# Mixture of experts: the last 128 tokens take slots behind each expert's first 128, and three quads of experts run in two passes

## The chip, the cores and the metric

One core of a Trainium2 chip runs the whole program in one launch. The metric is device time in microseconds (us) from start to end of that launch. The names of the engines in the profile: PE is TensorE (matrix products and transposes), PEld its weight loads, DVE is VectorE, ACT is ScalarE, POOL is GpSimd, SP is SyncE (it issues most DMA transfers). Each engine executes its own queue in order; the profile leaves buffer numbers out of the names of tiles.

## The reference

Six layers on x of 16 x 64 tokens by 256 channels. Five of them are untouched by this change. The last one is a mixture of experts, computed densely in the reference:

```python
def _gate(x, gate_w, gate_bias):          # 64 experts in 8 groups, 8 experts per token
    scores = jax.nn.sigmoid(x @ gate_w.T)
    sc = scores + gate_bias[None, :]
    # the 4 best groups by the sum of their two best scores; then the top 8 experts of these
    tw = jnp.take_along_axis(scores, tidx, axis=1)
    tw = tw / (tw.sum(-1, keepdims=True) + 1e-20)
    return (tidx, tw * 2.5)
def body(acc, ws):                        # once per expert
    wg, wu, wdn, cw = ws
    hmid = jax.nn.silu(x @ wg) * (x @ wu)
    return (acc + cw[:, None] * (hmid @ wdn), None)
y, _ = jax.lax.scan(body, jnp.zeros_like(x), (We_gate, We_up, We_down, w_dense.T))
shared = jax.nn.silu(hidden_states @ Ws_gate) * (hidden_states @ Ws_up) @ Ws_down
return y + shared                         # 1024 tokens, 256 channels, 128 hidden units per expert
```

## The kernel before

The kernel doesn't compute the 64 experts on all tokens. It sorts token rows by expert through two buffers in DRAM, `xbuf` and `ybuf`. The work of the last layer in order:

**Routing.** The 1024 tokens are eight groups of 128 (`NG` = 8, `P` = 128). `route(g)` normalises a group, computes scores, selects eight experts per token (`sel`, a 0/1 matrix of 128 tokens by 64 experts) and numbers the tokens of each expert. The number of a token within its expert is a sum: `before` (a triangular matrix of ones) times `sel` counts the tokens ahead of it in its own group, and `ones` times `seen` counts the tokens of all earlier groups, both accumulated in `ps_pos` (L1243 to L1246). `seen` is the running sum of `sel`. From this number comes the address of a row in `xbuf`, `idx` (L1255). `most` (L1261) is the largest count of any expert: if it were above `CAP` = 192, a dense fallback behind the loop would run. With these inputs it is not above that, before or after the change. `post` (L1160) issues GpSimd's indirect DMAs that scatter the token rows, one DMA per group and choice, 64 in all, with the list `scatters`.

**Slots.** Each expert has 192 slots. Four experts make a quad (16 quads); a quad has `NBLK` = 6 blocks of 128 rows: blocks 0 to 3 hold the first 128 slots of its four experts, block 4 the other 64 slots of its first two experts, block 5 those of the last two. Any group's tokens can land in any block.

**Experts.** `load_quad(q)` loads the weights of a quad (1.5 MB, `wq`, 5 buffers). `fetch(q)` (L1505) reads the quad's six blocks from `xbuf` into `xg` (3 buffers) in one DMA and is ordered behind all 64 scatters; it then computes on VectorE where each result row goes in `ybuf` (`mine`, `left`, `goal`). `turn(q, part)` (L1520) transposes two blocks on TensorE (four transposes) and copies them to `xT` (2 buffers): parts 0 and 1 by VectorE, part 2, the remainders, by ScalarE. `up(e)` (L1533) multiplies the gate and up weights of an expert with its 192 columns (`ps_ee`), applies Silu on ScalarE (`hg`) and multiplies on VectorE (`hT`). `down(e)` multiplies `hT` with the down weights: `ps_ey` for the first 128 slots of an expert, and for every second expert `ps_er` for the remainders of a pair, each half taking 64 partitions; results are copied to `yo` (4 buffers) and scattered to `ybuf` by GpSimd (`send`, L1547).

The loop at L1599 runs over the experts: at the start of a quad it fetches the quad after the next, in each of the next three iterations it does one part of the next quad's `turn`, then `up(e)` and `down(e - 3)`. Five quads of weights are loaded and two quads fetched ahead of it. `weights(g)` (L1581) computes the eight combine weights of a group's tokens on VectorE, four operations on 128 x 512 elements (L1584 eq, L1585 eq, L1587 w8, L1590 dgl); it is called from the same loop, every seventh expert:

```python
        if e % 7 == 3 and len(w8s) < NG:
            weights(len(w8s))
```

The order of each engine's queue is not the order of this text: a scheduler that works from dependencies and priorities places the instructions of all engines, and tile buffers add waits for the reader of an earlier tile. Behind the loop, `collect` and the code after it gather the eight result rows of each token from `ybuf` and sum them.

Of the kernel before, what the change touches and what calls it, by code (L numbers as in the profile page):

```python
# [34 lines left out]
CAP = 192  # L35
NBLK = 6
# [3 lines left out]
NOSLOT = 1 << 14  # L40

DX = D + 2 * TOPK

NAHEAD, NPE = 5, 4
BIG = 3.0e38
# [105 lines left out]
def perceiver_kernel(ctx: ExitStack, tc: tile.TileContext, a: dict, consts: bass.AP, out: bass.AP):  # L151
# [75 lines left out]
    def psb(shape, name):  # L227
        return ps_b.tile(shape, F32, tag="b", name=name)
# [3 lines left out]
    def after(i, others):  # L232
        for o in others:
            tc.add_manual_dep(i.ins, o.ins.name, mybir.DependencyInfo(mybir.DependencyClass.Sync, mybir.DependencyReason.DATA), reason="order")

# [941 lines left out]
    def route(g):  # L1177
# [23 lines left out]
        sc = tmp([P, E], "sc")  # L1201
        V.tensor_tensor(sc, sig, gb, ALU.add)


        scg = sc.rearrange("p (g k) -> p g k", k=8)
        hi, lo, n = scg, None, 4
# [33 lines left out]


        pp = psm([P, E], f"ps_pos_{g}")
        T.matmul(pp, lhsT=const2("before"), rhs=sel, start=True, stop=g == 0)  # L1243
        if g:
            T.matmul(pp, lhsT=const2("ones"), rhs=seen, start=False, stop=True)
        fit = tmp([P, E], "fit")  # L1246
        V.scalar_tensor_tensor(fit, pp, CAP - 0.5, sel, ALU.is_lt, ALU.mult)
# [8 lines left out]
        if g == NG - 1:  # L1256

            pn = psm([P, E], "ps_most")
            T.matmul(pn, lhsT=const2("ones"), rhs=seen, start=True, stop=False)
            T.matmul(pn, lhsT=const2("ones"), rhs=sel, start=False, stop=True)  # L1260
            V.reduce_max(most, pn, AX.X)  # L1261
        elif g == 0:
            V.tensor_copy(seen, sel)
        else:
            V.tensor_tensor(seen, seen, sel, ALU.add)
# [17 lines left out]
    with p2:  # L1283
# [168 lines left out]
        def shared():  # L1452
            w = loaded[0]
            wg, wu = (w[:, i * D : (i + 1) * D].rearrange("p (c f) -> p c f", c=2) for i in range(2))
            wd = w[:, 2 * D : 3 * D]
            for q in range(4):
                yield from until(lambda: sw["routed"] >= 2 * q + 2)
                tk = slice(q * 256, (q + 1) * 256)
                pe = psb([P, 2, 256], f"ps_se_{q}")
                for i, w in enumerate((wg, wu)):  # L1460
                    for c in range(2):
                        T.matmul(pe[:, i, :], lhsT=w[:, c, :], rhs=xnTm[:, c, tk], start=c == 0, stop=c == 1)
                th = wide("xth")([P, 256], f"th_s{q}")
                A.activation(th, pe[:, 0, :], AF.Tanh, scale=0.5)
# [23 lines left out]

    hid = ctx.enter_context(tc.tile_pool(name="hid", bufs=3, reuse_waits="tile"))

    wqs, xgs, goals, xTs, hTs, yos, pys = [], [], [], [], {}, {}, {}

    def wide_slot(name):
        return hid.tile([P, 4, 3 * D], F32, tag="wq", bufs=NAHEAD, name=name)
# [1 line left out]
    def load_quad(q):  # L1496

        w = wide_slot(f"wq_{q}")
        for i, n in enumerate(("gate", "up", "down")):
            v = a[f"L1_ffn_We_{n}"][4 * q : 4 * q + 4]  # L1500
            v = v.rearrange("e p d -> p e d") if i == 2 else v.rearrange("e (p c) f -> p e (c f)", c=2)
            nc.sync.dma_start(out=w[:, :, i * D : (i + 1) * D], in_=v)
        wqs.append(w)

    def fetch(q):  # L1505

        xg = hid.tile([P, NBLK, DX], F32, tag="xg", bufs=3, name=f"xg_{q}")
        after(nc.sync.dma_start(out=xg, in_=xbuf[q * QROWS : (q + 1) * QROWS, :].rearrange("(p s) d -> p s d", p=P)), scatters)
        mine = hid.tile([P, NBLK, TOPK], F32, tag="mine", bufs=2, name=f"mine_{q}")
        V.scalar_tensor_tensor(mine, xg[:, :, D : D + TOPK], float(q * QROWS), _bc(const2("own"), 2, TOPK), ALU.add, ALU.is_equal)  # L1510
        V.tensor_tensor(mine, mine, xg[:, :, D + TOPK : DX], ALU.mult)
        left = hid.tile([P, NBLK], F32, tag="left", bufs=2, name=f"left_{q}")
        V.reduce_sum(left, mine, AX.X)
        goal = hid.tile([P, NBLK], I32, tag="goal", bufs=4, name=f"goal_{q}")
        V.tensor_scalar(goal, left, -1.0, float(NOSLOT), ALU.mult, ALU.add)
        xgs.append(xg)
        goals.append(goal)
        xTs.append(hid.tile([P, 4, 2, CAP], F32, tag="xT", bufs=2, name=f"xT_{q}"))

    def turn(q, part):  # L1520

        pt = psb([P, 2, 2, P], f"ps_xT_{q}_{part}")
        xT = xTs[q]
        for s in range(2):
            for c in range(2):
                to = pt[:, c, s, :] if part == 2 else pt[:, s, c, :]
                T.transpose(to, xgs[q][:, 2 * part + s, c * P : (c + 1) * P], ident)  # L1527
        if part == 2:
            A.copy(xT[:, :, :, P:CAP].rearrange("p i c k -> p c i k"), pt.rearrange("p c s (u k) -> p c (s u) k", u=2))
        else:  # L1530
            V.tensor_copy(xT[:, 2 * part : 2 * part + 2, :, 0:P], pt)

    def up(e):  # L1533
        q, i = divmod(e, 4)
        pe = psb([P, 2, CAP], f"ps_ee_{e}")
        for j in range(2):
            for c in range(2):
                w = wqs[q][:, i, j * D + c * F : j * D + (c + 1) * F]
                T.matmul(pe[:, j, :], lhsT=w, rhs=xTs[q][:, i, c, :], start=c == 0, stop=c == 1)  # L1539
        hg = hid.tile([P, CAP], F32, tag="hg", name=f"hg_{e}")  # L1540
        A.activation(hg, pe[:, 0, :], AF.Silu)  # L1541
        hT = hid.tile([P, CAP], F32, tag="hT", bufs=5, name=f"hT_{e}")
        V.tensor_tensor(hT, hg, pe[:, 1, :], ALU.mult)
        hTs[e] = hT

    def send(y, goal):
        arr = G.indirect_dma_start(  # L1547
            out=ybuf,
            out_offset=bass.IndirectOffsetOnAxis(ap=goal, axis=0),
            in_=y,  # L1550
            in_offset=None,
            bounds_check=NTOK * TOPK - 1,
            oob_is_err=False,
        )

        if arrivals:
            tc.declare_no_dep(arr.ins, group="arrivals", reason="goals differ")
        tc.add_to_no_dep_group("arrivals", arr.ins)
        arrivals.append(arr)

    def down(e):
        q, i = divmod(e, 4)
        if i % 2 == 0:
            pys[e // 2] = psb([P, 2, D], f"ps_ey_{e}")
            yos[e // 2] = hid.tile([P, 3, D], F32, tag="yo", bufs=4, name=f"yo_{e}")
        py, yo = pys[e // 2], yos[e // 2]
        T.matmul(py[:, i % 2, :], lhsT=hTs[e][:, 0:P], rhs=wqs[q][:, i, 2 * D : 3 * D], start=True, stop=True)  # L1567
        if i % 2 == 0:
            return
        pr = psb([P, D], f"ps_er_{e}")  # L1570
        for u in range(2):
            T.matmul(pr[u * 64 : (u + 1) * 64, :], lhsT=hTs[e - 1 + u][:, P:CAP], rhs=wqs[q][:, i - 1 + u, 2 * D : 3 * D], start=True, stop=True)  # L1572
        A.copy(yo[:, 0:2, :], py)  # L1573
        V.tensor_copy(yo[:, 2, :], pr)
        for s in range(3):
            blk = i - 1 + s if s < 2 else 4 + i // 2
            send(yo[:, s, :], goals[q][:, blk : blk + 1])

# [13 lines left out]

    for q in range(NAHEAD):
        load_quad(q)
    fetch(0)
    fetch(1)
    for part in range(3):
        turn(0, part)
    for e in range(E + 3):  # L1599
        q, i = divmod(e, 4)  # L1600
        if i == 0 and q + 2 < NQUAD:
            fetch(q + 2)
        if i == 3 and q and q - 1 + NAHEAD < NQUAD:
            load_quad(q - 1 + NAHEAD)
        if e < E:
            if i < 3 and q + 1 < NQUAD:
                turn(q + 1, i)
            up(e)
        if e > 2:
            down(e - 3)  # L1610
        if e % 7 == 3 and len(w8s) < NG:
            weights(len(w8s))


# [87 lines left out]
```

## Time and profile before

| | before |
|---|---|
| median of 6 runs, us | 1088.95 (1084.83 to 1090.86) |
| profiled execution, us | 1087.79 |
| its span, first to last instruction, us | 1085.9 |
| mean granted TensorE clock | 0.915 |
| busy: PE / PEld / DVE | 858.5 (79%) / 648.6 (60%) / 632.7 (58%) |
| busy: ACT / POOL | 292.0 (27%) / 273.5 (25%) |
| `ps_ee` matmuls (L1539) | 512, 95.4 us busy |
| scatters to `xbuf` (L1163) / to `ybuf` (L1547) | 64, 69.5 us busy / 96, 93.7 us busy |
| first `ps_ee` | at 881.18 us |

Times in a timeline are microseconds from the start of the span. A row "busy, mean ns | idle before <-releaser" tells how long a group of instructions ran, and how long its engine had been idle just before them and what ended that. The experts lie from 881 to about 1043 us; the gather and the sum take the rest.

### The profile page before, as it was taken

Reading aid. Unit: us, or ns where it says so; the run is one execution under the profiler, and the core shown is the slowest. Engines: PE = TensorE matmul, PEld = TensorE weight load, DVE = VectorE, ACT = ScalarE, POOL = GpSimd, SP = SyncE. Lnnn points to the kernel's source line nnn. Section 1 sums busy time; section 2 is a strip of 40 time slices with the busy share of each in tenths; the row PEclk is TensorE's granted clock in tenths of the full one; section 3 lists DMA queues with packets and bytes.
Section 4 is the critical chain, followed back from the end, with each engine's and each line's share of the span. In section 5 each row is a group of like instructions: output and inputs, shape, how many; then the busy total and the mean of one; then the engine's idle time right before and its main releaser. Section 6 shows DMA issues by size and latency. Waiting matters only on the chain. (4 is left out here: it accounts for less than half of the span.)

```text
span 1085.9 us, 15921 instructions
## 1 busy us (share of the span) xinstructions
PE 858.5 (79%) x5858; PEld 648.6 (60%) x5858; DVE 632.7 (58%) x1863; ACT 292.0 (27%) x672; POOL 273.5 (25%) x302
## 2 busy tenths in 40 slices
PE   4878888978899788987786768877867369999945
PEld 3655565646656555655554556766766268777824
DVE  1446564565546564456556695979896853333316
ACT  0314032322233132231233454432311022232210
POOL 0000100001000101001011131575655516556540
PEclk8889999999999999999888788999998579999978
DMA  7411141310502131101501453343403859888236
GB/s 239 174 40 62 62 152 32 123 62 2 183 7 116 62 127 58 61 1 63 157 1 35 107 121 73 84 130 78 146 16 106 319 192 298 281 287 287 74 120 271
DMA packets 70725, 130.56 MB, mean 120 GB/s; under 512 B 10099, under 2 KB 56623, under 8 KB 67574
## 3 DMA queue, kind: packets, MB, share of 16 engines
q1 hardware_dynamic: 56016, 107.97, 30.6%
q0 software_dynamic: 7680, 17.33, 4.6%
q10 hardware_dynamic: 6950, 4.23, 1.4%
q8 instruction: 47, 0.77, 0.3%
q14 instruction: 32, 0.26, 0.1%
HBM read 97.54 MB, written 36.14 MB: 123 GB/s over the span
## 5 line engine op out<-in xcount | busy, mean ns | idle before, releaser
L1547 POOL DMA_INDIRECT ybuf<-yo,goal x96 | 93.7, 976 | 85.8 <-ACT yo L1573 31.1
L1539 PE MATMUL ps_ee<-xT,wq 128*128 128x192 f32 x512 | 95.4, 330 | 0.0
L1539 PEld LDWEIGHTS ps_ee<-xT,wq 128*128 128x128 f32 x512 | 81.8, 190 | 6.5 <-issue 3.5
L1163 POOL DMA_INDIRECT xbuf<-xtok,idx x64 | 69.5, 1086 | 47.9 <-issue 16.8
L994 PE MATMUL fpy<-fw,fxm 128*128 128x256 f32 x256 | 60.6, 397 | 13.3 <-DVE fxm L991 6.8
L630 PE MATMUL po_a<-cn,paT_a 128*64 128x256 f32 (+1 forms) x416 | 57.0, 410 | 15.7 <-ACT paT_a L624 7.7
L994 PEld LDWEIGHTS fpy<-fw,fxm 128*128 128x128 f32 x256 | 50.4, 199 | 24.3 <-issue 16.0
L1400 PE MATMUL ps_g<-pc,pb 128*128 128x128 f32 x384 | 55.1, 306 | 9.7 <-DVE pb L1367 6.7
L1400 PEld LDWEIGHTS ps_g<-pc,pb 128*128 128x128 f32 x384 | 53.2, 220 | 12.8 <-POOL pc L1369 10.7
L630 PE MATMUL po_b<-cn,paT_b 128*64 128x256 f32 (+1 forms) x416 | 50.2, 385 | 9.2 <-DVE paT_b L624 8.3
L208 POOL TENSOR_TENSOR rs_ff<-ve_ff,neghalf 128x1 f32<-128x1 f32 x8 | 4.4, 550 | 209.4 <-DVE ve_ff L206 197.9
L404 PE MATMUL psc<-ct,cn 128*128 128x128 f32 x384 | 49.8, 280 | 3.6 <-DVE cc_a L570 2.2
L1541 ACT ACTIVATE hg<-ps_ee 128x192 f32<-128x192 f32 x64 | 21.3, 333 | 109.0 <-PE ps_ee L1539 40.6
L592 PE MATMUL sc_b<-cT,qT_b 128*64 128x512 f32 (+1 forms) x256 | 47.3, 524 | 2.1 <-DVE qT_b L564 1.6
L630 PEld LDWEIGHTS po_a<-cn,paT_a 128*64 128x64 f32 (+1 forms) x416 | 28.5, 145 | 33.5 <-ACT paT_a L624 8.7
L404 PEld LDWEIGHTS psc<-ct,cn 128*128 128x128 f32 x384 | 44.7, 145 | 6.4 <-issue 3.2
L197 ACT COPY cT<-psc 128x512 f32<-128x512 f32 x51 | 29.8, 589 | 63.9 <-PE psc L404 63.3
L1527 PE MATMUL ps_xT<-ct,xg 128*128 128x128 f32 x192 | 30.7, 288 | 20.2 <-DMA xg<-xbuf 20.2
L592 PE MATMUL sc_a<-cT,qT_a 128*64 128x512 f32 (+1 forms) x256 | 46.4, 505 | 0.0
L630 PEld LDWEIGHTS po_b<-cn,paT_b 128*64 128x64 f32 (+1 forms) x416 | 27.7, 136 | 25.4 <-DVE paT_b L624 10.1
L208 POOL TENSOR_TENSOR rs_ml<-ve_ml,neghalf 128x1 f32<-128x1 f32 x8 | 5.6, 705 | 141.8 <-DVE ve_ml L206 141.8
L1527 PEld LDWEIGHTS ps_xT<-ct,xg 128*128 128x128 f32 x192 | 24.1, 148 | 28.7 <-DMA xg<-xbuf 20.4
(443 smaller groups left out, 1888.2 us busy)
## 6 DMA issues: line engine op xcount, KB each, us to landing
cn<-in_ctx_dram SPq DMA_DIRECT2D x16, 1536.0 KB
e<-segd SPq DMA_DIRECT2D x16, 896.0 KB
xbuf<-zero SPq DMA_DIRECT2D x8, 1632.0 KB
xg<-xbuf SPq DMA_DIRECT2D x16, 816.0 KB
wq<-in_L_ffn_We_gate_dram SPq DMA_DIRECT2D x16, 512.0 KB
wq<-in_L_ffn_We_up_dram SPq DMA_DIRECT2D x16, 512.0 KB
wq<-in_L_ffn_We_down_dram SPq DMA_DIRECT2D x16, 512.0 KB
yg<-ybuf SPq DMA_DIRECT2D x8, 1024.0 KB
```

The source lines that it names most:

```text
L197: A.copy(dst, src)
L208: root = G.tensor_tensor(rs, ve, neghalf[:, 0:1], ALU.pow)
L404: T.transpose(ps[:, j, :], cn[:, 4 * q + j, c * P : (c + 1) * P], ident)
L592: T.matmul(sc[b * 64 : (b + 1) * 64, :], lhsT=qT[:, c, b * 64 : (b + 1) * 64], rhs=cTs[2 * g + b][:, c, 512 * j : 512 * j + n], start=c == ...
L630: T.matmul(pos[j > 0][b * 64 : (b + 1) * 64, :], lhsT=paTs[j][:, i, b * 64 : (b + 1) * 64], rhs=cns[2 * g + b][0:r, k, :], start=k in (0, ...
L994: T.matmul(py, lhsT=xm[:, t, c, :], rhs=fw[:, 2 * h + t, c, :], start=h + t + c == 0, stop=h == 3 and t == 1 and c == 1,)
L1163: sct = G.indirect_dma_start(out=xbuf, out_offset=bass.IndirectOffsetOnAxis(ap=idx[:, g, k : k + 1], axis=0), in_=xtok[:, g, 0:DX], in_off ...
L1400: T.matmul(pg[:, 2 * j : 2 * j + 2, :].rearrange("p q t -> p (q t)"), lhsT=pb[:, l + i, j, :], rhs=pcs[l + i][:, j, :, :].rearrange("p q t ...
L1527: T.transpose(to, xgs[q][:, 2 * part + s, c * P : (c + 1) * P], ident)
L1539: T.matmul(pe[:, j, :], lhsT=w, rhs=xTs[q][:, i, c, :], start=c == 0, stop=c == 1)
L1541: A.activation(hg, pe[:, 0, :], AF.Silu)
L1547: arr = G.indirect_dma_start(out=ybuf, out_offset=bass.IndirectOffsetOnAxis(ap=goal, axis=0), in_=y, in_offset=None, bounds_check=NTOK * T ...
```

## The change

Three things. First, the last group's tokens are numbered from `full` = max(128, tokens of earlier groups), so that they take slots behind each expert's first 128, that is only in blocks 4 and 5. Second, the first three quads (`NSPLIT` = 3, twelve experts) are done in two passes: blocks 0 to 3, whose fetch is ordered behind the first 56 scatters only, with `up` on columns 0 to 128 and the `ps_ey` products; then blocks 4 and 5, fetched behind all scatters, into a tile of their own, with `up` on columns 128 to 192 and the `ps_er` products. The main loop starts at expert 12. Third, the first Silu is ordered behind the shared expert's last Tanh, the first send behind the last scatter in GpSimd's queue, and `weights` is called every sixth expert. The declaration with "rows" says that a first-pass fetch reads other blocks than the last group's scatters write.

```diff
+NSPLIT = 3
...
+        if g == NG - 1:                                # in route(g)
+            pn = psm([P, E], "ps_full")
+            T.matmul(pn, lhsT=const2("ones"), rhs=seen, start=True, stop=True)
+            full = tmp([P, E], "full")
+            V.tensor_scalar(full, pn, float(P), None, ALU.max)
...
-        T.matmul(pp, lhsT=const2("before"), rhs=sel, start=True, stop=g == 0)
-        if g:
+        last = g == NG - 1
+        T.matmul(pp, lhsT=const2("before"), rhs=sel, start=True, stop=last or g == 0)
+        if last:
+            pos = tmp([P, E], "pos")
+            V.tensor_tensor(pos, pp, full, ALU.add)
+            pp = pos
+        elif g:
             T.matmul(pp, lhsT=const2("ones"), rhs=seen, start=False, stop=True)
...
-            T.matmul(pn, lhsT=const2("ones"), rhs=seen, start=True, stop=False)
-            T.matmul(pn, lhsT=const2("ones"), rhs=sel, start=False, stop=True)
-            V.reduce_max(most, pn, AX.X)
+            T.matmul(pn, lhsT=const2("ones"), rhs=sel, start=True, stop=True)
+            V.tensor_tensor(full, full, pn, ALU.add)
+            V.reduce_max(most, full, AX.X)
...
-    def fetch(q):
-        xg = hid.tile([P, NBLK, DX], F32, tag="xg", bufs=3, name=f"xg_{q}")
-        after(nc.sync.dma_start(out=xg, in_=xbuf[...]), scatters)
+    def fetch(q, lo=0, hi=NBLK):                       # xg, goal: only blocks lo to hi
+        ld = nc.sync.dma_start(out=xg, in_=rows)
+        if hi == 4:
+            after(ld, scatters[:-TOPK])
+            tc.declare_no_dep(ld.ins, group="rows", keep=[o.ins for o in scatters[:-TOPK]], reason="blocks differ")
+        else:
+            after(ld, scatters)
...
+        if part == 2 and q < NSPLIT:                   # in turn(q, part)
+            xT = xTs[q] = hid.tile([P, 4, 2, CAP], F32, tag="xT", bufs=2, name=f"xTr_{q}")
...
-    def up(e):
+    def up(e, lo=0, hi=CAP):                           # only columns lo to hi
...
+        if e == 0 and lo == 0:
+            after(silu, [sw["tanh"]])
...
+        if not arrivals:                               # in send
+            behind(arr, scatters[-1])
...
-    def down(e):
+    def down(e, first=True, rest=True):                # first: ps_ey; rest: ps_er
...
-    fetch(0)
-    fetch(1)
-    for part in range(3):
-        turn(0, part)
-    for e in range(E + 3):
+    for q in range(NSPLIT):
+        fetch(q, 0, 4)
+    n = 4 * NSPLIT
+    for e in range(n + 2):
+        if e < n:
+            if e % 4 == 0:
+                turn(e // 4, 0)
+                turn(e // 4, 1)
+            up(e, 0, P)
+        if e > 1:
+            down(e - 2, rest=False)
+    for q in range(NSPLIT):
+        fetch(q, 4, NBLK)
+    for e in range(n + 2):
+        if e < n:
+            if e % 4 == 0:
+                turn(e // 4, 2)
+                if e:
+                    load_quad(e // 4 - 1 + NAHEAD)
+            up(e, P, CAP)
+        if e > 1:
+            down(e - 2, first=False)
+    load_quad(NSPLIT - 1 + NAHEAD)
+    fetch(NSPLIT)
+    fetch(NSPLIT + 1)
+    for part in range(3):
+        turn(NSPLIT, part)
+    for e in range(n, E + 3):
...
-        if i == 3 and q and q - 1 + NAHEAD < NQUAD:
+        if i == 3 and q > NSPLIT and q - 1 + NAHEAD < NQUAD:
...
-        if e > 2:
+        if e > n + 2:
             down(e - 3)
-        if e % 7 == 3 and len(w8s) < NG:
+        if e % 6 == 3 and len(w8s) < NG:
```

In a second pass `ps_er` of a pair is made in two separate iterations, one half each, where before both halves stood next to each other.

More of the change, by code (lines that the diff above doesn't have):

```diff
@@ L234, in after, with behind @@
             tc.add_manual_dep(i.ins, o.ins.name, mybir.DependencyInfo(mybir.DependencyClass.Sync, mybir.DependencyReason.DATA), reason="order")
+    def behind(i, o):
+        tc.add_manual_dep(i.ins, o.ins.name, mybir.DependencyInfo(mybir.DependencyClass.NoSync, mybir.DependencyReason.DATA), reason="order")
     def drive(*kinds):
@@ L1463, in shared @@
                 th = wide("xth")([P, 256], f"th_s{q}")
-                A.activation(th, pe[:, 0, :], AF.Tanh, scale=0.5)
+                sw["tanh"] = A.activation(th, pe[:, 0, :], AF.Tanh, scale=0.5)
                 hT = wide("xc")([P, 256], f"hT_s{q}")
@@ L1489, in perceiver_kernel @@
     hid = ctx.enter_context(tc.tile_pool(name="hid", bufs=3, reuse_waits="tile"))
-    wqs, xgs, goals, xTs, hTs, yos, pys = [], [], [], [], {}, {}, {}
+    wqs, xgs, goals, xTs, hTs, yos, pys, prs = [], [], [], [], {}, {}, {}, {}
     def wide_slot(name):
@@ L1503, in load_quad @@
         wqs.append(w)
-    def fetch(q):
-        xg = hid.tile([P, NBLK, DX], F32, tag="xg", bufs=3, name=f"xg_{q}")
-        after(nc.sync.dma_start(out=xg, in_=xbuf[q * QROWS : (q + 1) * QROWS, :].rearrange("(p s) d -> p s d", p=P)), scatters)
-        mine = hid.tile([P, NBLK, TOPK], F32, tag="mine", bufs=2, name=f"mine_{q}")
-        V.scalar_tensor_tensor(mine, xg[:, :, D : D + TOPK], float(q * QROWS), _bc(const2("own"), 2, TOPK), ALU.add, ALU.is_equal)
+    def fetch(q, lo=0, hi=NBLK):
+        if lo == 0:
+            xgs.append(hid.tile([P, NBLK, DX], F32, tag="xg", bufs=3, name=f"xg_{q}"))
+            goals.append(hid.tile([P, NBLK], I32, tag="goal", bufs=4, name=f"goal_{q}"))
+            xTs.append(hid.tile([P, 4, 2, CAP], F32, tag="xT", bufs=2, name=f"xT_{q}"))
+        xg, goal = xgs[q][:, lo:hi, :], goals[q][:, lo:hi]
+        rows = xbuf[q * QROWS : (q + 1) * QROWS, :].rearrange("(p s) d -> p s d", p=P)[:, lo:hi, :]
+        ld = nc.sync.dma_start(out=xg, in_=rows)
[4 more added lines that the diff above has]
+            after(ld, scatters)
+        mine = hid.tile([P, NBLK, TOPK], F32, tag="mine", bufs=2, name=f"mine_{q}_{lo}")[:, lo:hi, :]
+        V.scalar_tensor_tensor(mine, xg[:, :, D : D + TOPK], float(q * QROWS), _bc(const2("own")[:, lo:hi], 2, TOPK), ALU.add, ALU.is_equal)
         V.tensor_tensor(mine, mine, xg[:, :, D + TOPK : DX], ALU.mult)
-        left = hid.tile([P, NBLK], F32, tag="left", bufs=2, name=f"left_{q}")
+        left = hid.tile([P, NBLK], F32, tag="left", bufs=2, name=f"left_{q}_{lo}")[:, lo:hi]
         V.reduce_sum(left, mine, AX.X)
-        goal = hid.tile([P, NBLK], I32, tag="goal", bufs=4, name=f"goal_{q}")
         V.tensor_scalar(goal, left, -1.0, float(NOSLOT), ALU.mult, ALU.add)
-        xgs.append(xg)
-        goals.append(goal)
-        xTs.append(hid.tile([P, 4, 2, CAP], F32, tag="xT", bufs=2, name=f"xT_{q}"))
     def turn(q, part):
@@ L1531, in turn @@
             V.tensor_copy(xT[:, 2 * part : 2 * part + 2, :, 0:P], pt)
-    def up(e):
+    def up(e, lo=0, hi=CAP):
         q, i = divmod(e, 4)
-        pe = psb([P, 2, CAP], f"ps_ee_{e}")
+        pe = psb([P, 2, CAP], f"ps_ee_{e}_{lo}")[:, :, lo:hi]
         for j in range(2):
@@ L1538, in up @@
                 w = wqs[q][:, i, j * D + c * F : j * D + (c + 1) * F]
[L1539 to L1543, printed above, removed]
+                T.matmul(pe[:, j, :], lhsT=w, rhs=xTs[q][:, i, c, lo:hi], start=c == 0, stop=c == 1)
+        hg = hid.tile([P, CAP], F32, tag="hg", name=f"hg_{e}_{lo}")[:, lo:hi]
+        silu = A.activation(hg, pe[:, 0, :], AF.Silu)
+        if e == 0 and lo == 0:
+            after(silu, [sw["tanh"]])
+        hT = hid.tile([P, CAP], F32, tag="hT", bufs=5, name=f"hT_{e}_{lo}")
+        V.tensor_tensor(hT[:, lo:hi], hg, pe[:, 1, :], ALU.mult)
         hTs[e] = hT
@@ L1559, in send @@
         arrivals.append(arr)
-    def down(e):
+    def down(e, first=True, rest=True):
         q, i = divmod(e, 4)
         if i % 2 == 0:
[L1564 to L1567, printed above, removed]
+            if first:
+                pys[e // 2] = psb([P, 2, D], f"ps_ey_{e}")
+            yos[e // 2] = hid.tile([P, 3, D], F32, tag="yo", bufs=4, name=f"yo_{e}_{rest}")
+        yo = yos[e // 2]
+        if first:
+            py = pys[e // 2]
+            T.matmul(py[:, i % 2, :], lhsT=hTs[e][:, 0:P], rhs=wqs[q][:, i, 2 * D : 3 * D], start=True, stop=True)
+        if not first and i % 2 == 0:
+            prs[e // 2] = psb([P, D], f"ps_er_{e}")
+        if not first:
+            u = i % 2
+            T.matmul(prs[e // 2][u * 64 : (u + 1) * 64, :], lhsT=hTs[e][:, P:CAP], rhs=wqs[q][:, i, 2 * D : 3 * D], start=True, stop=True)
         if i % 2 == 0:
             return
[L1570 to L1575, printed above, removed]
+        if first:
+            A.copy(yo[:, 0:2, :], py)
+        if rest:
+            if first:
+                pr = psb([P, D], f"ps_er_{e}")
+                for u in range(2):
+                    T.matmul(pr[u * 64 : (u + 1) * 64, :], lhsT=hTs[e - 1 + u][:, P:CAP], rhs=wqs[q][:, i - 1 + u, 2 * D : 3 * D], start=True, stop=True)
+            else:
+                pr = prs[e // 2]
+            V.tensor_copy(yo[:, 2, :], pr)
+        for s in range(0 if first else 2, 3 if rest else 2):
             blk = i - 1 + s if s < 2 else 4 + i // 2
```

## The prediction

> **What bounds the kernel now.** I read the windows (the stretch where the gap is), then the timeline there, then the groups of the VectorE queue, then the timeline of one pair of experts at full clock for prices. First the windows from 840 us; columns: stretch, length, busy us with instruction counts of PE, PEld, DVE, ACT, POOL, granted PE clock, DMA share, GB/s.
>
> ```profile
> 850.00:858.00 8.00, 1.94 (x8) 1.78 (x8) 7.63 (x28) 0.00 (x0) 3.60 (x4) 0.50 1.08 392
> 858.00:877.00 19.00, 0.00 (x0) 0.00 (x0) 15.70 (x29) 0.00 (x0) 9.40 (x8) 0.50 0.56 192
> 879.00:881.00 2.00, 2.00 (x11) 1.90 (x9) 1.73 (x6) 0.46 (x1) 0.00 (x0) 0.54 0.80 336
> 881.00:883.00 2.00, 1.96 (x14) 1.80 (x13) 1.35 (x5) 1.63 (x3) 0.00 (x0) 1.00 0.75 238
> 896.00:916.00 20.00, 20.00 (x125) 16.73 (x125) 7.30 (x25) 5.85 (x14) 11.60 (x12) 1.00 0.89 289
> ```
>
> TensorE does nothing for 19 us while GpSimd issues the last scatters; but VectorE is busy 15.70 of those 19 us. Later, in the experts, TensorE is busy 20.00 of 20 us: there the end is set by TensorE work, so TensorE time added there is added to the kernel. The timeline of the gap (start, duration, engine, line; in brackets the idle time before and its releaser):
>
> ```profile
> 859.86 1.93 POOL L1163 DMA_INDIRECT xbuf<-xtok,idx  x1 [5.34 <-DVE idx L1255]
> ...
> 870.42 0.97 POOL L1163 DMA_INDIRECT xbuf<-xtok,idx  x1 [0.30 <-issue]
> ...
> 873.05 7.75 SPq L1508 DMA_DIRECT2D xg<-xbuf  x4
> 873.52 0.69 DVE L1590 TENSOR_TENSOR dgl<-ct,w 128x512 f32<-128x512 f32 x1
> 877.61 0.21 DVE L1510 SCALAR_TENSOR_TENSOR mine<-xg,ct 128x48 f32<-128x48 f32 x1 [3.40 <-DMA xg<-xbuf]
> 877.63 3.51 PE L1527 MATMUL ps_xT<-ct,xg 128*128 128x128 f32 x16 [20.23 <-DMA xg<-xbuf]
> ```
>
> So the first expert waits for: last idx 859.42, eight scatters to 871.39, fetch 873.05, landed 877.6. The dgl row beside it is the other thing to see. It is the last of the combine weights (`weights`), which the text of the kernel puts into the expert loop, but which VectorE executes here, in one run (VectorE groups, 849.9 to 874.3; busy us, mean ns of one, then idle before):
>
> ```profile
> L1590 DVE TENSOR_TENSOR dgl<-ct,w 128x512 f32<-128x512 f32 x8 | 5.5, 689 | 0.2
> L1585 DVE TENSOR_TENSOR eq<-eq,wt 128x512 f32<-128x512 f32 x8 | 5.5, 686 | 0.2
> ```
>
> With L1584 and L1587, equally long, these are 32 rows of 0.69 us, 22 us, ending at 874.21. In before they cost nothing: the data comes at 877.6.
>
> **The start.** After the change the first fetch waits for 56 scatters only (the last of these ended at 854.52) and can land about 4.5 us after its issue, early in the gap. TensorE turns its eight blocks, but their copy into `xT` (new line 1559) is VectorE's, and in the built order of the changed kernel the VectorE queue reads: `idx` of the last group, then 26 of the 32 `weights` rows (new L1629 to L1635), and only then `mine` (L1540), `left`, `goal` and the copy. An engine's queue is executed in order, so the first expert waits for VectorE, not for data. VectorE's work to that point is the 32 rows as before plus three new 128x64 operations (pos, full twice), at 0.13 start to start (847.60 to 847.74) about 0.3: free at 874.21+0.3 = 874.5. Then 0.9 for mine/left/goal (877.61 to 878.5 in before), 0.69 for the copy, 0.1 to TensorE: first `ps_ee` at 876.2 instead of 881.18: **-5.0**. The other bound is no `weights` rows in the way: rival A.
>
> The remainder's fetch isn't late: 5 `weights` rows fewer stand ahead of the last `idx` (6, before 11), so idx comes about 3 us earlier, 856.5, and eight scatters later (11.5 us), 868, the second fetch goes out; it is needed when the first pass ends: twelve `up` of 0.94, twelve `ps_ey` of 0.5, sixteen transposes of 0.11 and 1.7 for the clock (all below) after 876.2, that is 897. The route's extra TensorE product and the three DVE rows are in those numbers; `ps_pos` and `ps_most` each have one product fewer: 0.
>
> **Transposes.** Before, sixteen transposes were done ahead of 881.18; after, eight. The other eight at 0.11 come later: **+0.9**. In before the half clock (0.50 to 879, 0.54 to 881) ended with those transposes. After the change TensorE again comes from a gap of over 10 us, so expert work runs at half clock for the 3.4 us that the transposes needed (877.63 to 881): 0 if the early transposes count, at most half of 3.4, 1.7. I take **+1.7**, the row nearest.
>
> **The split matmuls.** Twelve experts do `up` twice, 128 and 64 columns wide, instead of once with 192. Prices at full clock:
>
> ```profile
> 801.09 2.03 PE L1357 MATMUL ps_C<-xnTm,winT 128*128 128x128 f32 x16
> 802.96 1.90 PE L1433 MATMUL ps_y<-xtok,gt 128*128 128x64 f32 x16
> 804.69 1.94 PE L1382 MATMUL ps_z<-winT,xnTm 128*128 128x512 f32 x4
> ...
> 897.99 1.47 PE L1539 MATMUL ps_ee<-xT,wq 128*128 128x192 f32 x8
> 899.29 0.59 PE L1567 MATMUL ps_ey<-wq,hT 128*128 128x256 f32 x2
> 899.82 0.65 PE L1572 MATMUL ps_er<-wq,hT 128*64 128x256 f32 x4
> 900.40 0.66 PE L1527 MATMUL ps_xT<-ct,xg 128*128 128x128 f32 x4
> ```
>
> Start to start: 192 wide, 1.30 for 8 (0.163 each); 128 wide, 1.87/16 = 0.117; 64 wide, 1.73/16 = 0.108. So 64 columns cost nearly as much as 128: each has a 128x128 weight load to go with it, and below 128 columns that load is the floor. An expert: 8 x (0.113+0.108) = 1.77 against 1.30, +0.47; twelve: **+5.6**. Bounds: +0.5 if 64 columns cost half of 128 (8 x (0.113+0.057) = 1.36 each, +0.06); +7.3 with 0.117 and a little gap each (+0.61).
>
> [...]
>
> **The rest products.** `ps_er` before: the two halves of a pair go side by side in 0.58 for four instructions (899.82 to 900.40). In the second pass another `up` stands between the halves, so each runs alone, nearest row `ps_ey`, two of 256 columns in about 0.5: 1.0 for 0.58, six pairs, **+2.4** (1.7 at 0.43, 3.0 at 0.54).
>
> **Exposed copies.** Before, the transposes of quad q+1 are spread over quad q. In the split passes they stand directly ahead of their use. First pass, quads 1 and 2: VectorE copy 0.69, partly covered by the pending `down`, 0.45 each. Second pass, three turns with ScalarE copies (0.59 plus 0.3 to and from it, and behind the `yo` copy on ScalarE): about 1.05, 0.85, 0.9. **+3.7** (2 to 5.5).
>
> **Nothing for:** ACT_TABLE_LOAD (1.28 at 881.15, begun beside the first `ps_ee`): after, it waits for that matmul's end, and `down` follows two experts later, so the second expert's matmuls and transposes cover 1.3; uncovered it is +1.4. [...] The other new waits hold nobody: the first Silu waits for the shared expert's Tanh, which was done before 846.19 (VectorE reads it there), and the first send stands behind the last scatter, over by 868, while no result exists before 880. The sends stay 96, and 11.60 of 20 us busy leaves GpSimd room. Later stage: 0, bounds in the rivals.
>
> **Sum:** -5.0+0.9+1.7+5.6+2.4+3.7 = +9.3. On the profiled 1087.79 (span 1085.9 and 1.9 around it) that is 1097.1; the median of the runs, 1088.95, stands 1.2 higher. I say 1097. A measurement of this kernel can tell about 0.3%, 3.3 us, from no change.
>
> **Rivals.**
>
> A, *it starts early as the scatters allow*: the copies aren't held by `weights`. From 854.52, 1.7 to the issue (871.39 to 873.05), 4.6 to landing (873.05 to 877.61), 1.7 to the matmul as above and one row of 0.69 in between: first `ps_ee` at 863.2 or a little later, I say 863.6, 12.6 before my 876.2. 9.3-12.6 = -3.3: 1084.5, faster. For it: data and expert weights are there. Against: the built queue, and the rows of before, which run in just such an order. It decides if the new L1540 runs before the L1629 to L1635 rows. 0.06.
>
> B, *most of it given back later*: between 916 and 1036 TensorE is idle for 5.06 us (18.24 of 20 busy in 916 to 936, DMA share 0.84), because weights and blocks arrive late. With the start spread, the queued loads get further ahead, and that idle goes: 9.3-5.1 = +4.2, 1092. The low end of the split price gives the same, 9.3-5.6+0.5 = +4.2; both together, -0.9, no change. Against the first: the transfers are as many and their buffers come free later too. 0.13.
>
> C, *slower still, one queue*: SyncE's transfers are issued in order. In the built order wq_5, wq_6, wq_7 (each waiting for a quad's second pass) stand ahead of xg_5 to xg_7; before, weights and blocks alternated (wq_5 at 895.83, an xg at 903.26). wq_7 goes out when the second pass ends, about 918; three loads of 1.5 MB at 290 GB/s are 5.4 us each, so xg_5 may land around 926, when VectorE's queue reaches its `mine`, with the copies for the next quad behind that. TensorE then waits 4 to 8: 1101 to 1105. Against: in before TensorE never lost over 1.8 in 20 us to this. It decides if xg_5 lands after 926. 0.12.
>
> **How the numbers follow.** Forecast 0.69, A 0.06, B 0.13, C 0.12. The forecast's unknowns: split +0.5 to +7.3, half clock 0 to 1.7, copies 2 to 5.5, table 0 to 1.4; not all at one end, about 1091 to 1101. The range takes in B and C: 1087 to 1105; A lies outside. Faster by over 0.3% (below 1085.7): A and a sliver of B and of the forecast's low end, 0.10. Within: most of B and the low end of the forecast, 0.13. Slower (above 1092.2): 0.77.
>
> **What would show it.** In the profile after: first `ps_ee` about 876, released by DVE xT, just after a dgl row; 128x64 `ps_ee` groups at 0.108 each; GpSimd's scatters over by 868; the first expert of quad 3 at about 919 (907.75 before). Wrong if `ps_ee` starts before 870, if 64-wide rows take under 0.08, or if TensorE's idle after 916 is not near 5.

## The result and the profile after

The changed kernel takes 1100.08 us (median of 20 runs, 1093.41 to 1109.86) against 1089.93 for the kernel before (46 runs): a ratio of 1.0087, 95% interval 1.0071 to 1.0104, which is 9.5 us more. The ratio leaves out the one slow run, 1109.86 us at a mean granted clock of 0.895. The profiled execution took 1097.9 us with a span of 1095.7, 9.8 more than before.

Because the layers ahead of the change vary from one execution to the next, I read the traces from one point on: the first `more` row of the last group on VectorE (the ranking of the expert groups in `route(7)`), "the ranking" below. It comes at 847.60 before and at 849.79 after. From there to the end of the last `ps_er` it is 196.28 us before and 204.55 after: +8.3. The 2.2 ahead of the ranking and -0.7 behind the experts make up the rest of the 9.8.

First the windows of the changed kernel, columns as before:

```profile
858.00:877.00 19.00, 1.94 (x8) 1.57 (x8) 18.28 (x34) 0.00 (x0) 8.78 (x8) 0.50 0.91 339
879.00:881.00 2.00, 2.00 (x11) 2.00 (x11) 1.39 (x10) 1.08 (x1) 0.00 (x0) 0.50 0.00 0
881.00:883.00 2.00, 2.00 (x14) 1.95 (x14) 0.57 (x2) 1.03 (x4) 0.00 (x0) 0.77 0.00 0
900.00:920.00 20.00, 18.52 (x122) 13.97 (x122) 5.12 (x23) 3.61 (x14) 6.82 (x7) 1.00 0.64 200
```

In the 19 us in which TensorE did nothing it now does eight transposes, 1.94 us. VectorE is busy 18.28 of 19 us, before 15.70. The half clock lasts 2 us longer than before. In the second pass TensorE is not even busy all the time (18.52 of 20). The timeline of the start (new line numbers: L1170 scatter, L1532 fetch, L1555 and L1559 `turn`, L1567 `up`, L1635 the last row of `weights`):

```profile
861.49 13.66 SPq L1532 DMA_DIRECT2D xg<-xbuf  x6
868.28 1.19 POOL L1170 DMA_INDIRECT xbuf<-xtok,idx  x1 [0.30 <-issue]
870.00 1.94 PE L1555 MATMUL ps_xT<-ct,xg 128*128 128x128 f32 x8 [13.69 <-DMA xg<-xbuf]
875.65 0.69 DVE L1635 TENSOR_TENSOR dgl<-ct,w 128x512 f32<-128x512 f32 x1
876.26 0.18 DVE L1540 SCALAR_TENSOR_TENSOR mine<-xg,ct 128x32 f32<-128x32 f32 x1
877.00 0.69 DVE L1559 COPY xT<-ps_xT 128x512 f32<-128x512 f32 x1
877.74 4.92 PE L1567 MATMUL ps_ee<-xT,wq 128*128 128x128 f32 x24 [5.80 <-DVE xT L1559]
879.92 1.28 ACT L1569 ACT_TABLE_LOAD   x1 [30.96 <-PE ps_ee L1567]
```

The first blocks are there at 870.0, when the last scatter has only just been issued (868.28 and 1.19); the copy that the first expert needs starts at 877.00, directly behind the last dgl row and four rows of `mine`, `left` and `goal`. TensorE's bracket says the same from the other side: 5.80 us idle, ended by VectorE's xT.

The prices of the two passes, from the timeline of TensorE at full clock, first two rows of the first pass, then of the second:

```profile
882.93 1.05 PE L1567 MATMUL ps_ee<-xT,wq 128*128 128x128 f32 x8
883.83 0.60 PE L1602 MATMUL ps_ey<-wq,hT 128*128 128x256 f32 x2
...
906.48 1.10 PE L1567 MATMUL ps_ee<-xTr,wq 128*128 128x64 f32 x8 [0.68 <-ACT xTr L1557]
907.51 0.65 PE L1607 MATMUL ps_er<-wq,hT 128*64 128x256 f32 x2
908.09 1.10 PE L1567 MATMUL ps_ee<-xTr,wq 128*128 128x64 f32 x8
```

Start to start: eight 128 columns wide 0.90, eight 64 columns wide 1.03, one half of `ps_er` 0.58. An expert's `up` costs 0.89+1.03 where before it cost 1.30.

### The profile page after: what moved, and what is told of

It is laid out like the page before. It is cut to its first block, busy times and chain, and to the rows that moved or that the text cites. A ratio compares the mean times of both kernels' runs of the same rounds, so it can differ in the third digit from the quotient of the medians.

```text
span 1095.7 us, 16171 instructions
## 1 busy us (share of the span) xinstructions
PE 874.4 (80%) x5952; PEld 661.5 (60%) x5952; DVE 637.1 (58%) x1890; ACT 295.6 (27%) x684; POOL 270.8 (25%) x302
## 4 chain that ended last, share of the span: by engine, by line
PE 50%; DVE 24%; DMA 10%; issue 8%; ACT 4%; POOL 2%; ACTq 0%; POOLq 0%; SPq 0%; another core or an unknown queue 0%; DVEq 0%
PE fpy L1001 5%; PE po_b L637 4%; PE sc_b L599 4%; PE po_a L637 4%; PE sc_a L599 4%; PE ps_ee L1567 4%; PE psc L411 3%; PE ps_g L1419 2%; POOL ybuf L1577 2%; DMA ybuf<-yo_True,goal 2%; DMA xg<-xbuf 2%; DVE pc L1388 1%; DVE gs L1229 1%; DMA x<-in_x_dram 1%; DVE gt L1427 1%
## 5 line engine op out<-in xcount | busy, mean ns | idle before, releaser
L1577 POOL DMA_INDIRECT ybuf<-yo_True,goal x84 | 81.9, 976 | 75.6 <-issue 21.5
L1567 PE MATMUL ps_ee<-xT,wq 128*128 128x192 f32 (+1 forms) x512 | 92.1, 325 | 6.8 <-DVE xT L1559 6.2
L1567 PEld LDWEIGHTS ps_ee<-xT,wq 128*128 128x128 f32 x512 | 80.5, 196 | 13.3 <-DVE xT L1559 6.8
L1170 POOL DMA_INDIRECT xbuf<-xtok,idx x64 | 67.0, 1047 | 44.2 <-issue 16.8
L1569 ACT ACTIVATE hg<-ps_ee 128x192 f32<-128x192 f32 (+2 forms) x76 | 23.2, 307 | 109.8 <-PE ps_ee L1567 75.8
L1573 DVE TENSOR_TENSOR hT<-hg,ps_ee 128x192 f32<-128x192 f32 (+2 forms) x76 | 23.7, 319 | 50.0 <-ACT hg L1569 45.6
L1555 PE MATMUL ps_xT<-ct,xg 128*128 128x128 f32 x192 | 29.8, 283 | 14.8 <-DMA xg<-xbuf 14.8
```

The lines of the kernel that those rows point to most:

```text
L1170: sct = G.indirect_dma_start(out=xbuf, out_offset=bass.IndirectOffsetOnAxis(ap=idx[:, g, k : k + 1], axis=0), in_=xtok[:, g, 0:DX], in_off ...
L1567: T.matmul(pe[:, j, :], lhsT=w, rhs=xTs[q][:, i, c, lo:hi], start=c == 0, stop=c == 1)
L1569: silu = A.activation(hg, pe[:, 0, :], AF.Silu)
L1573: V.tensor_tensor(hT[:, lo:hi], hg, pe[:, 1, :], ALU.mult)
L1577: arr = G.indirect_dma_start(out=ybuf, out_offset=bass.IndirectOffsetOnAxis(ap=goal, axis=0), in_=y, in_offset=None, bounds_check=NTOK * T ...
```

## Experiments

Every ratio below is against runs of the kernel before on the same chip; the medians themselves differ between chips (before: 1077 to 1090 us), so only ratios are compared. Times in the three right columns come from one profile each, in us.

| kernel | ratio, 95% interval | ranking to first `ps_ee` | first `ps_ee` to last `ps_er` | ranking to last `ps_er` |
|---|---|---|---|---|
| before | 1 | 33.6 | 162.7 | 196.3 |
| before, second profile | - | 32.4 | 163.7 | 196.1 |
| changed | 1.0087 (1.0071 to 1.0104) | 28.0 | 176.6 | 204.6 |
| after_wait_all | 1.0091 (1.0064 to 1.0117) | 27.8 | 178.6 | 206.4 |
| after_late | 1.0072 (1.0044 to 1.0099) | 20.9 | 178.0 | 199.0 |
| before_slots | 0.9974 (0.9954 to 0.9995) | 29.4 | 162.7 | 192.0 |
| before_late | 0.9979 (0.9956 to 1.0003) | 27.0 | 160.4 | 187.4 |
| after_pairs | 1.0185 (1.0157 to 1.0213) | 27.9 | 180.8 | 208.7 |
| after_hoist | 1.0087 (1.0058 to 1.0116) | 27.8 | 171.1 | 198.9 |
| after_wide | one run | 27.9 | 175.6 | 203.5 |
| pairs_wide | one run | 27.9 | 174.8 | 202.7 |
| p1_all | 0.9969 (0.9943 to 0.9996) | 15.9 | 172.3 | 188.2 |
| p2_hoist | 0.9980 (0.9955 to 1.0005) | 14.0 | 176.3 | 190.2 |
| p3_hoist | 1.0003 (0.9975 to 1.0032) | 16.0 | 176.9 | 192.9 |

My theory going in: VectorE's queue holds the first blocks, and the passes then cost TensorE time. The rivals: data or scatters hold them; the loss is in the routing; the loss comes later, from transfers.

### Is it the early fetch, VectorE's queue or the numbering?

**after_wait_all**: the first fetches wait for all scatters.

```diff
         if hi == 4:
-            after(ld, scatters[:-TOPK])
-            tc.declare_no_dep(ld.ins, group="rows", keep=[o.ins for o in scatters[:-TOPK]], reason="blocks differ")
+            after(ld, scatters)
```

> The changed kernel, with the first fetches ordered behind all 64 scatters instead of the first 56. Theory: VectorE is held to 876.3 anyway, and the scatters end near 869, so the fetch lands by about 876: the total moves by less than 1.5 us, that is, the early fetch as such brings next to nothing in the changed kernel. Rival (the early fetch does bring the start forward): 4 us slower or more.

```profile
873.04 1.94 PE L1554 MATMUL ps_xT<-ct,xg 128*128 128x128 f32 x8 [18.51 <-DMA xg<-xbuf]
875.87 5.49 PE L1566 MATMUL ps_ee<-xT,wq 128*128 128x128 f32 x24 [0.89 <-DVE xT L1558]
```

The timeline of TensorE in this kernel: the transposes come 25.0 us after the ranking (873.04 less 848.04), 4.8 later than in the changed kernel, and yet the first `ps_ee` stands 27.8 us after the ranking as there (28.0). The idle time in the bracket has shrunk from 5.80 to 0.89: only the wait for VectorE became shorter. The ratio is the same. Fetching early brings nothing in the changed kernel.

**after_late**: the combine weights behind the experts that they are written beside.

```diff
-        V.tensor_tensor(hT[:, lo:hi], hg, pe[:, 1, :], ALU.mult)
+        sw["hT"] = V.tensor_tensor(hT[:, lo:hi], hg, pe[:, 1, :], ALU.mult)
...
-        V.tensor_tensor(eq, _bc(key[:, g, :], 1, TOPK), _bc(k8[:, g, :], 2, E), ALU.is_equal)
+        behind(V.tensor_tensor(eq, _bc(key[:, g, :], 1, TOPK), _bc(k8[:, g, :], 2, E), ALU.is_equal), sw["hT"])
```

> The changed kernel with the combine weights (32 VectorE rows) ordered behind the expert they are written beside. Theory (VectorE's queue holds the first blocks): the first ps_ee no longer follows a dgl row but the landing of xg, which in the changed kernel's trace is at 869.9; it starts near 872 instead of 877.7, and the total falls by about 5.6 us, to some 1.004 of before. Rival 1 (the data or the clock hold it): start and total move by less than 1 us. Rival 2 (the early start is given back by the wait for the second fetch or by VectorE rows among the experts): start near 872, total within 2 us of the changed kernel.

```profile
852.84 11.58 SPq L1532 DMA_DIRECT2D xg<-xbuf  x6
860.97 1.94 PE L1555 MATMUL ps_xT<-ct,xg 128*128 128x128 f32 x8 [14.46 <-DMA xg<-xbuf]
862.09 0.69 DVE L1559 COPY xT<-ps_xT 128x512 f32<-128x512 f32 x1 [0.39 <-PE ps_xT L1555]
862.84 3.39 PE L1567 MATMUL ps_ee<-xT,wq 128*128 128x128 f32 x19
```

VectorE now waits for TensorE (0.39), not the reverse, and the start is 7 us earlier after the ranking. So the queue did hold the blocks. Up to the last `ps_er` 5.6 us of it are left. The ratio moved less than that, by 0.0015 with intervals of 0.003 on each side: the size is not settled by the times. Nor is the traced run typical: it took 1085.23 us, the other five 1093 to 1101. A second limit shows: the fetch needs 8.1 us from its issue (852.84) to its landing (860.97), where before it needed 4.6. The weight loads of five quads are issued just ahead of it; that they are the reason is tried in the last kernels below.

**before_slots**: only `route` taken from the changed kernel, in the kernel before.

```diff
-        T.matmul(pp, lhsT=const2("before"), rhs=sel, start=True, stop=g == 0)
+        last = g == NG - 1
+        T.matmul(pp, lhsT=const2("before"), rhs=sel, start=True, stop=last or g == 0)
...
```

> The kernel before with only the numbering of the last 128 tokens changed; no passes, no early fetch. Theory: the added operations cost nothing, and six instead of eleven combine-weight rows stand ahead of the last idx in the queue, so the last scatters begin about 1.3 us earlier: 0.998 to 1.000 of before. Rival (the numbering itself costs, by the longer chain from sel to idx): 0.5 to 2 us slower.

No cost: 0.9974. The last `idx` comes 8.3 us after the ranking instead of 11.8; in the queue five `weights` rows fewer stand ahead of it, 5 x 0.69 = 3.5. The gain is larger than the 1.3 I had expected, since I had read it from absolute times of two executions. So the numbering alone brings the first `ps_ee` to 29.4 us after the ranking. The early fetch and the two passes bring it 1.4 us further, to 28.0, and spend 13.9 us more from there on (176.6 for 162.7).

**before_late**: the kernel before with the combine weights behind the experts, by the same edit as above.

> The kernel before with the same order for the combine weights and nothing else. Theory: eleven of these rows stood ahead of the last idx and made it late; GpSimd, idle 5.3 us ahead of its last eight scatters, then begins them at about 854.8 instead of 859.9, and everything behind moves up by about 5 us: 0.995 of before. Rival 1 (GpSimd's scatters or the weight transfers set the landing of xg, not idx): less than 1 us. Rival 2 (the rows cost more among the experts than beside the scatters): no gain, or up to 2 us slower.

The last `idx` follows the ranking by 6.5 us (860.19 less 853.65), 5.3 less than before, as the theory has it. GpSimd begins the last scatters at 860.63. The time has 0.9979 with an interval that includes 1; the 0.995 that I expected lies just outside it. The second profile of the kernel before (**before_again**, unchanged) was run to see whether the first profile had been a bad measure:

> The kernel before, unchanged, for a profile on the same chip as the two kernels beside it. Theory: from the last group's ranking to the last expert's result it takes 196 us as in the first profile, with the last idx some 11.8 us after the ranking. Rival (those 11.8 us were particular to that execution): the last idx comes 8 to 10 us after the ranking, and the gains read from single traces against the first profile are too large by as much.

It had not: 196.1 after 196.3 from ranking to last result, and the last `idx` 10.9 us after the ranking. What stays open is why gains of 4 to 9 us between these points in single traces come out as 2 to 3 us in the medians, or as none. They are not given back behind the experts: from the last `ps_er` to the end of the span it is 40.8 to 43.0 us in all fourteen profiles. The ranking itself lies anywhere from 839.5 to 853.7 us in these profiles.

### What do the two passes cost?

**after_pairs**: both halves of `ps_er` next to each other in the second pass.

```diff
-        if not first:
-            u = i % 2
-            T.matmul(prs[e // 2][u * 64 : (u + 1) * 64, :], lhsT=hTs[e][:, P:CAP], rhs=wqs[q][:, i, 2 * D : 3 * D], start=True, stop=True)
+        if not first and i % 2:
+            for u in range(2):
+                T.matmul(prs[e // 2][u * 64 : (u + 1) * 64, :], lhsT=hTs[e - 1 + u][:, P:CAP], rhs=wqs[q][:, i - 1 + u, 2 * D : 3 * D], start=True, stop=True)
```

> The changed kernel with the two ps_er halves of a pair put next to each other again in the second pass. Theory: twelve single halves of 0.57 us start to start become six pairs of 0.58, so 3.4 us go: some 1.005 to 1.006 of before, where the changed kernel has 1.0087. Rival (the halves' cost lies elsewhere, for instance in the wait for hT): less than 1 us, or a new wait of the pair for the second hT.

It became slower by a further 10 us by the ratio (in the trace by 4.2, from ranking to last result). The window of the second pass (columns as in the first fence) and one group of its timeline:

```profile
900.00:920.00 20.00, 18.65 (x82) 14.79 (x78) 4.42 (x18) 2.52 (x8) 3.89 (x4) 0.50 0.46 131
```

```profile
902.23 3.67 PE L1567 MATMUL ps_ee<-xTr,wq 128*128 128x64 f32 x16 [0.68 <-ACT xTr L1557]
905.83 1.12 PE L1607 MATMUL ps_er<-wq,hT 128*64 128x256 f32 x4
```

The granted clock is 0.50 although TensorE is busy for 18.65 of 20 us. A pair of halves takes 1.05 at half clock. The clock was at 1.00 in the changed kernel's second pass, where, behind the first 24, a `ps_er` half stood between every eight narrow matmuls; here 32 and then 16 stand in a row. **pairs_wide** asks whether their width does it. The second pass computes columns 64 to 192; the added 64 columns hold a copy and are not used.

```diff
             A.copy(xT[:, :, :, P:CAP].rearrange("p i c k -> p c i k"), pt.rearrange("p c s (u k) -> p c (s u) k", u=2))
+            if q < NSPLIT:
+                A.copy(xT[:, :, :, 64:P].rearrange("p i c k -> p c i k"), pt.rearrange("p c s (u k) -> p c (s u) k", u=2))
...
-            up(e, P, CAP)
+            up(e, 64, CAP)
```

> The changed kernel with ps_er in pairs, where the granted clock fell to 0.50 from about 897 to 922 us, and with the second pass 128 columns wide instead of 64 (the added columns hold a copy and are not used). Theory 1 (the clock follows how much TensorE streams: rows of 64 columns leave it half empty): the clock stays at 1.00 in the second pass, eight matmuls take about 0.9, and the second pass is some 7 us shorter than the 30 us with 64 columns although twice the columns are computed. Theory 2 (the clock follows gaps or the pattern of instructions): it falls to 0.50 here too.

```profile
900.00:920.00 20.00, 17.43 (x133) 13.91 (x133) 8.97 (x31) 5.47 (x16) 6.64 (x7) 1.00 0.85 278
```

```profile
903.88 2.05 PE L1569 MATMUL ps_ee<-xTr,wq 128*128 128x128 f32 x16 [1.16 <-ACT xTr L1559]
905.87 0.65 PE L1609 MATMUL ps_er<-wq,hT 128*64 128x256 f32 x4
```

With twice the columns, and less busy (17.43), the clock stays at 1.00: sixteen matmuls take 1.99 instead of 3.60 us, a pair of halves 0.58. So between these two runs, one profile each, the clock went with the columns that TensorE streamed, not with whether it had an instruction. And the pairs do save what was expected: 0.58 instead of 1.15 for two halves.

**after_wide** is the same widening without the pairs.

> The changed kernel with the second pass 128 columns wide instead of 64 (columns 64 to 192; the added 64 columns hold a copy of the remainder's, made by one more ScalarE copy per quad, and their results are not used). Theory (the weight load is the floor of a narrow matmul): eight matmuls of 128 columns take no longer than eight of 64, that is 0.9 to 1.03 us start to start as in the first pass. Rival (columns cost): 64 columns took less than half of the price of 128 plus a wait, and the eight go up by 0.4 us or more.

In the timeline of TensorE, eight of 128 columns between two `ps_er` halves take 1.09 start to start (893.81 to 894.90), eight of 64 took 1.03 in the changed kernel: half of the columns save 6%, and the rival's 0.4 is far off. But the same eight of 128 columns took 0.90 in the first pass. What is new is the neighbour, a product with 64-column weights.

**after_hoist**: the transposes of the next quad one quad earlier.

```diff
-            if e % 4 == 0:
-                turn(e // 4, 0)
-                turn(e // 4, 1)
+            q, i = divmod(e, 4)
+            if e == 0:
+                turn(0, 0)
+                turn(0, 1)
+            if i in (1, 2) and q + 1 < NSPLIT:
+                turn(q + 1, i - 1)
+            if e == n - 2 and NSPLIT > 1:
+                fetch(0, 4, NBLK)
+                turn(0, 2)
             up(e, 0, P)
...
-            if e % 4 == 0:
-                turn(e // 4, 2)
-                if e:
-                    load_quad(e // 4 - 1 + NAHEAD)
+            if i == 0 and e:
+                load_quad(q - 1 + NAHEAD)
+            if i == 2 and q + 1 < NSPLIT:
+                turn(q + 1, 2)
             up(e, P, CAP)
```

> The changed kernel with the transposes of the next quad moved into the experts of the quad before it, in both passes. Theory: TensorE's idle time in the two passes, 0.7 and 2.5 us in the changed kernel's trace, is the exposed copy of xT; 2.5 of the 3.2 us go. Rival 1 (copies are then late behind other VectorE and ScalarE rows): less than 1 us. Rival 2: the gain is real in the passes and given back later, since quad 3 then waits for its blocks.

In the trace the waits for xT and xTr between quads are gone, and ranking to last result is 198.9, 5.7 less. The ratio, on another chip, is that of the changed kernel. Of the trace's gain nothing is shown by the times.

### What if nothing held the first blocks?

Three kernels put it together: combine weights late, the loads of the fourth and fifth quad's weights behind the first fetches, and one, two or three quads in two passes. p1_all has `ps_er` in pairs; p2_hoist and p3_hoist have the transposes ahead and the halves apart.

```diff
-NSPLIT = 3
+NSPLIT = 1
...
-    for q in range(NAHEAD):
+    for q in range(3):
         load_quad(q)
     for q in range(NSPLIT):
         fetch(q, 0, 4)
+    for q in range(3, NAHEAD):
+        load_quad(q)
```

> One quad in two passes instead of three, the combine weights behind their experts, the loads of the fourth and fifth quad's weights behind the first fetch, ps_er halves together. Theory: with VectorE free and the transfer queue shorter, the first ps_ee comes some 17 us after the last group's ranking (the first more row) instead of 33.6 before and 28 in the changed kernel; the split of four experts costs 2.5, the half clock 2: some 10 us faster than before, 0.989 to 0.993. Rival 1 (the second fetch or the weights of quads 1 to 4 come too late): TensorE waits after the first pass and the gain is under 4 us. Rival 2 (what is saved at the start comes back as waits for transfers among the later experts): start as in the theory, total gain under 4 us.

> Two quads in two passes; combine weights behind their experts, the fourth and fifth quad's weights behind the first fetches, transposes moved ahead, ps_er halves apart as in the changed kernel. Theory: the first ps_ee comes some 16 us after the last group's ranking, as with one quad in two passes (15.9 there); two quads in the first pass reach past the landing of the second fetch, so the 4.3 us in which TensorE waited there go; no run of 32 narrow matmuls without a ps_er between, so the granted clock stays at 1.00 in the second pass. Some 10 us faster than before, 0.987 to 0.994. Rival 1 (the narrow matmuls of any second pass drop the clock): clock near 0.5 in the second pass, no faster than with one quad. Rival 2 (the rest of the experts then waits for transfers): start as said, gain under 4 us.

> As the kernel with two quads, with three. This is the change as it was meant, with what held it taken away. Theory: start as with two quads; four more experts pay the split (0.9 us each), so 2 to 4 us slower than with two, and 5 to 8 us faster than before: 0.992 to 0.996. Rival (a longer first pass gives the weight loads time, later waits go): as fast as with two quads.

The starts are as expected, 14 to 16 us after the ranking, 17.6 to 19.6 earlier than before; with fewer weight loads ahead of it the first fetch lands 4.4 us after its issue (862.82 to 867.17 in p3_hoist). The totals are not: 0.9969, 0.9980, 1.0003. In p1_all TensorE waited 3.6 us for the second fetch and its clock was 0.52 from 870 to 880, with 32 narrow matmuls in a row behind that wait; in p2_hoist it waited 2.1 us for the first hT and, among the later experts, another 6.0 us for hT, as the kernel before does (4.8 and 2.4). p3_hoist is the change as it is described, unhindered. Three of its TensorE rows:

```profile
869.04 2.08 PE L1567 MATMUL ps_ee<-xT,wq 128*128 128x128 f32 x8
890.82 1.89 PE L1567 MATMUL ps_ee<-xTr,wq 128*128 128x64 f32 x16
892.55 0.60 PE L1555 MATMUL ps_xT<-ct,xg 128*128 128x128 f32 x4
```

It starts 17.6 us earlier than before and spends 176.9 instead of 162.7 us from there to the last `ps_er`: 14.2 are given back, in the trace 3.4 are left, and the time shows none of it. The middle row also has the narrow matmul without a `ps_er` half beside it: 16 in 1.73, 0.108 each.

No version is faster by more than a few tenths of a per cent; the best, p1_all and before_slots, have intervals that end just under 1.

## Why the prediction was right, step by step

The forecast, 1097 us or 9.3 over the profiled run, stands against +9.5 by the ratio and +8.3 between ranking and last result. The mechanism of the start came as forecast; that the sum came so close is in part luck, since two errors cancel. Its terms:

- **The start, -5.0**: measured -5.6 from the ranking (33.6 to 28.0), for the reason given: the dgl row, four small rows, the copy. after_wait_all and after_late show that it is VectorE's queue. In absolute time it was 877.74, not 876.2, because the ranking came 2.2 later.
- **Transposes +0.9 and half clock +1.7**: the first 24 matmuls take 4.76 (877.74 to 882.50) for 3 x 0.89, so +2.1, a little over the upper bound of 1.7; the early transposes did not wake the clock. Behind gaps of 13.7 and 5.8 us it stood at 0.50 to 881 and at 0.77 in the two us after that.
- **Split +5.6**: first passes 12 x 0.89; second passes 9 x 1.03, and 2.83 for the first three experts, which stand together (900.13 to 902.96); less 12 x 1.30: +7.2, at the top of the bounds +0.5 to +7.3. The floor was right: 64 columns cost 0.108 alone (p3_hoist, 16 in 1.73), exactly the row of `ps_y`, and no 64-wide row came near the 0.08 that would have shown it wrong. The weight loads beside the two rows of before agree: PEld was busy 1.87 us for the 16 of `ps_y`, 64 columns wide, as for the 16 of `ps_C`, 128 wide. The sum missed that each eight stand between products with 64-column weights.
- **Rest products +2.4**: ten halves alone and one pair, as two halves ended up together at the end of the pass (920.12), 6.33 in all, less 6 x 0.58: +2.9, just inside the upper bound of 3.0. The rows go with the weights of the neighbour: 0.13 rather than 0.108 per narrow matmul with a half on each side (1.03 for eight), 0.108 where the neighbours have 128-column weights too (p3_hoist), and 0.58 for the half where `ps_ey`, with as many columns and 128-column weights, takes 0.43. No row times a half without a product with 128-column weights beside it, and why such a neighbour costs is not shown.
- **Exposed copies +3.7**: TensorE's idle time in the passes is 0.7 and 2.5, together 3.2. With the terms above that makes 16.3 of the 17.1 below; the other 0.8 is in no term.
- **Table load 0**: hidden, as the first `ps_ee` ran on. The load of 1.28 us ended at 881.20 and the first Silu began at 881.21.
- **Later stage 0**: from the first expert of quad 3 to the last `ps_er` it is 130.5 after; before, 907.75 to 1043.88 less 2.45 of pending `down` work (three `ps_ey` at 0.43, two pairs of `ps_er` at 0.58), 133.7: 3.2 given back. But it is not rival B's idle time that went. TensorE's idle time among the experts is still near 5, as the prediction said it must be: 4.84 from 923.86 on, against 5.06 before from 916 to 1036. What went is mostly the wait of 2.38 for the last expert's hT before (1042.60), which some of the other kernels have and some lack; nothing here shows why. B also had the reason of that idle time wrong. Before, 4.8 of it is released by hT, and in the three waits of over 1 us VectorE stood at a `goal` row ahead of hT that waited for a send, as at 925.75:

```profile
925.75 0.17 DVE L1515 TENSOR_SCALAR goal<-left 128x6 int32<-128x6 f32 x1 [6.23 <-DMA ybuf<-yo,goal]
```

- **Rival C**: its sign came, its price did not. The `mine` row of xg_5 starts at 932.11, later than 926, and TensorE waited 1.15 us there for the fetch, not 4 to 8.

The passes thus cost 17.1 instead of 14.3 (877.74 to 923.86 where quad 3 begins, against 881.18 to 907.75 and the pending 2.45), and 3.2 come back later: two errors of about 3 us that cancel. Sum: -5.6+17.1-3.2 = +8.3. So quad 3 began at 923.86 and not at about 919, 2.2 of that for the later ranking and 2.8 for the passes.

Rival A was mis-sized in one number: with VectorE free the first `ps_ee` comes at 20.9 us after the ranking (after_late), 7 and not 12.6 earlier, since the first fetch took 8.1 us to land and not the 4.6 of before. With the loads of two quads issued behind it (p3_hoist) it landed in 4.4, and the first `ps_ee` came 12 us earlier than in the changed kernel; that points to the weight loads.

## What to carry to other kernels

Before work is moved into a gap, look at what the engines of its whole chain do in that gap: TensorE was idle for 19 us, but the copy that it needed stood behind 26 rows of another engine's queue, put there by a scheduler because nothing forbade it. And splitting a matmul's columns to start earlier is paid on TensorE at once: here a matmul of 64 columns took 0.108 us where one of 128 took 0.117, and in this stage, which TensorE bounds (busy 20.00 of 20 us from 896 to 916 before), 12 experts in two passes cost 17 us, nearly all that the earliest start for them was worth (17.6, p3_hoist). Read a change of a few us from a fixed event of its own stage, and hold it against medians before it is believed.

## What the runs showed of the hardware that I had not expected

- The granted clock can fall to 0.50 while TensorE is busy: 18.65 of 20 us in after_pairs, with rows of 64 columns one behind another; with 128 columns in their place it stayed at 1.00 at 17.43 busy. How long such a stretch lasts may have a part too: with 24 narrow matmuls in a row (2.83 us) the changed kernel kept 1.00, and with 16 (1.73 us) p3_hoist did, while p1_all, with 32 behind a wait of 3.6 us, stood at 0.52 from 870 to 880 and took 7.02 us for the 32. As an estimate from the rows, the run that lost the clock streamed 64/0.108 = 590 columns per us at its start, the changed kernel's second pass, which kept it, (8 x 64 + 2 x 256)/1.61 = 640. No run separates what part the columns, the length of the stretch and the `ps_er` halves in between have in it.
- The clock lost this way in after_pairs cost more than what the edit saved: the second pass took 30 us (893.35 to 923.51) instead of 23 (898.81 to 921.98), although its instructions were some 3 us cheaper at full clock (as an estimate, six pairs at the 0.58 of pairs_wide where twelve halves took 1.15 for two).
- In the changed kernel, products with 64-column weights between products with 128-column ones cost both of them: as an estimate from the rows (1.03 for 8 x 0.108, and 0.58 for the 0.43 of `ps_ey`), about 0.16 us for each change between the two at full clock.
